# Moving layer norms and one inverse in a two-block transformer kernel: places in cross-attention, self-attention and SyncE's queue

## The chip, the cores and the metric

The kernel runs on one core of a Trainium2 chip. The metric is device microseconds of one execution. Five engines work side by side and meet at semaphores: TensorE (PE; weight loads are listed apart as PEld), VectorE (DVE), ScalarE (ACT), GpSimd (POOL) and SyncE (SP, which here only issues DMAs). Each runs its own list of instructions in order. In the profile SPq and ACTq are DMA-issuing instructions of SP and ACT.

## The reference

All of it is float32, x is 8 batches of 512 rows of 256. Two blocks follow each other; the change is in the second:

```python
attn_in = _adaln(x, cond, ln1_w, ...)      # layer norm, then (1 + g) * . + b from cond
x = _attn(attn_in, attn_in, sa_wq, sa_wkv, sa_wo, sa_bo) + x      # 16 heads of 64, rope on q and k
cross_in = _adaln(x, cond, ln1_w, ...)
ctx_n = _ln(context, ca_lnc_w, ca_lnc_b)   # 64 context rows of 192 per batch
x = _attn(cross_in, ctx_n, ca_wq, ca_wkv, ca_wo, ca_bo) + x
ffn_in = _adaln(x, cond, ln2_w, ...)
h = gelu(ffn_in @ ff_w1 + ff_b1)
x = h @ ff_w2 + ff_b2 + x
```

Each `_attn` divides its softmax numerators by their sums. The kernel applies exp without a row maximum, sums the exponentials with matmuls, and multiplies by the inverse of the sums later.

## The kernel before, in words

All eight x[b] stay in SBUF as 128 x 4 x 256 (512 rows in 4 tiles of 128). Within the second block the order of every engine's instructions is the order of the Python calls (a manual schedule); only a few loads outside it (the weights w_ff1 and w_ff2, both listed as w_ff_w, L140) are put into SP's list by the planner, where their buffers come free.

**A norm and its way to PE.** Statistics, rstd (a power on POOL, L158) and the product z (L191 in pieces, L170 in one) are 128 rows by 256 columns; PE wants the columns on the partitions. `blocks_turned` (L410) transposes 32 x 32 blocks on DVE (L413), writes them to HBM with four DMAs (`turned_d`, L416) and reads them back with one (`z<-turned_d`, L418), both on SP. `modulated` (L424, hT at L427) applies scale and shift on ACT. `normed_in_pieces` (L431) gives the norm as three pieces: statistics of two tiles; statistics of the other two and rstd; the product. `add_row` (L446) adds a bias row to x on POOL afterwards.

**Self-attention** (`slots`, L1125) goes through batches b and, in each, through four groups g of four heads. Per group: scores, exponentials on ACT, sums of the exponentials (sm) on DVE and POOL, values, and `sums` (L1065): four matmuls, a copy den on ACT, a DMA to HBM (den_d) and one back as 128 x 16 (rec). One group later `inverse` (L1083) takes the reciprocal on DVE, writes it to HBM (rec_d) and fetches it spread over partitions (rb, four DMAs), and `scaled` (L1100) multiplies oT by rb, half on DVE, half on POOL. All of these DMAs are on SP, except for those of the last group of the last batch, which `queue` (L1062) puts on ACT. Within batch b the norm of batch b+1 runs in pieces at g = 0, 0 and 1, and its modulation (`turn`) at g = 2.

**Between self-attention and cross-attention** the lines after the loop set the order by hand: cross_values 1 to 3 (the values of the context, copied on ACT to a tile v, written by SP to HBM as v_d), the norms of batches 0 and 1, the last group's inverse, the output projection of the last batch (`last_out`, first heads 0 to 5 of 8 pairs, then 6 and 7, which need the last inverse), the first two pieces of batch 2's norm. The tiles v and the turned blocks share the tag "t" with two buffers. `load_vb(0)` fetches the values back as kv.

**Cross-attention** (`cross`, in `fast_path`, L1369 on) has for each batch b eight places j = 0 to 7. Each place holds one query matmul group, six ahead of its use (`queries(8*b + j + 6)`), with rope on DVE (L846, L847) and POOL (L851, L852). Around them:

- j = 0: sums(b-1, 1), score(b, 0), two `outer` (values by output weights, copied to vw on ACT), scaled(b-1, 0)
- j = 1: turn(b+1), two `outer`, inverse(b-1, 1)
- j = 2: the first query that reads the hT of batch b+1; load_kb(b+1), load_vb(b+1)
- j = 4: sums(b, 0), score(b, 1), scaled(b-1, 1)
- j = 5, 6, 7: cross_out(b-1, t) with t = 0; 1; 2 and 3; then rows_(b+2, n) with n = 0, 1, 2, the three pieces of the norm of batch b+2 (for b = 6 and 7: of the feed-forward's batches 0 and 1)
- j = 6 also, behind those: inverse(b, 0)

Here sums, inverse and scaled go the same way over HBM, with two den DMAs (L1290), one rec (L1292), one rec_d (listed as `rec<-rec`, L1299), eight rb (L1304) and four products p<-p,rb (L1311), the odd ones on DVE, the even ones on POOL. cross_out (`ps<-vw,p`) sums over eight p, those of half 1 last. PSUM banks of queries, outer, sums and cross_out go round in the order D, O, X, X.

## Time and profile before

| | |
|---|---|
| median of 3 runs | 2320.97 us (2315.08 to 2325.16) |
| profiled execution | 2323.46 us, of which the span is 2321.6 us |
| granted TensorE clock, mean | 0.989 |
| first block | to about 804 us |
| self-attention of the second block | 804 to 1731 us |
| transition | 1731 to 1770 us |
| cross-attention | 1770 to about 2065 us, then feed-forward to the end |

A line of the timeline reads: start, duration, engine and line, operation, out<-in, count, and in brackets how long the engine had been idle before and what released it. PE busy counts modelled ends of pipelined matmuls. One float32 matmul appears as two records.

### The profile page before, as it was taken

The numbers are of one execution on the slowest core, as the hardware profiler recorded it, in microseconds if no ns is written. First come the engines' busy times: TensorE is split into PE (matmuls) and PEld (weight loads), VectorE is DVE, ScalarE is ACT, GpSimd is POOL, SyncE is SP. The second block draws the span as 40 slices with busy tenths as digits, with TensorE's granted clock in tenths as the row PEclk, the third lists the DMA queues.
The fourth block names the chain that finished last, engine by engine and source line by source line (L and its number), as shares of the span: only waits on it lengthen the run. The fifth ranks groups of instructions, "written<-read, shape, count | busy, mean of one in ns | idle before, by whom it ended". The sixth has DMA issues, their size and how long they took to land.

```text
span 2321.6 us, 30915 instructions
## 1 busy us (share of the span) xinstructions
PE 2274.8 (98%) x12180; PEld 1153.6 (50%) x12180; DVE 1113.9 (48%) x1935; ACT 864.8 (37%) x1309; POOL 922.6 (40%) x584
## 2 busy tenths in 40 slices
PE   9999999999999999999999999999998899999998
PEld 4444554554545533434343434343444455567665
DVE  5676555565555454444444444444434554442220
ACT  4566455455542134242424242424241221221221
POOL 4652333333210056454545454545443444432110
PEclk9999999999999999999999999999999999999999
DMA  6120000000002001010101010101033333322221
GB/s 191 34 96 6 12 6 8 12 6 7 3 10 75 18 15 38 20 38 20 38 19 38 20 38 19 38 20 38 20 96 106 103 94 86 103 73 79 55 62 35
DMA packets 106267, 104.16 MB, mean 45 GB/s; under 512 B 39185, under 2 KB 80897, under 8 KB 106113
## 3 DMA queue, kind: packets, MB, share of 16 engines
q1 hardware_dynamic: 104632, 98.92, 14.9%
q8 instruction: 98, 1.61, 0.3%
q0 software_dynamic: 576, 2.10, 0.2%
q10 hardware_dynamic: 904, 1.07, 0.2%
q14 instruction: 57, 0.46, 0.1%
HBM read 79.96 MB, written 22.09 MB: 44 GB/s over the span
## 4 chain that ended last, share of the span: by engine, by line
PE 91%; DVE 3%; DMA 3%; POOL 1%; issue 1%; SPq 1%; ACT 0%; ACTq 0%; DVEq 0%; POOLq 0%
PE ps_P L88 40%; PE ps_B L88 30%; PE ps_X L88 7%; PE ps_S L88 5%; PE ps_D L88 4%; PE ps_O L88 2%; DMA z<-turned_d 1%; DMA turned_d<-hT 1%; PE ps_B L566 1%; DVE z L191 1%; SPq L416 1%; PE ps_B L406 1%; POOL var L557 1%; PE ps_B L598 1%; DVE hT L413 0%
## 5 line engine op out<-in xcount | busy, mean ns | idle before, releaser
L615 ACT ACTIVATE p<-ps_B 128x512 f32<-128x512 f32 x576 | 292.1, 622 | 163.8 <-PE ps_B L88 163.8
L1036 ACT ACTIVATE p<-ps_P 128x1024 f32<-128x1024 f32 x256 | 244.8, 1025 | 90.9 <-PE ps_P L88 90.9
L88 PE MATMUL ps_P<-q,k 32*128 32x512 f32 x2048 | 238.9, 600 | 1.4 <-DVE t L1015 1.4
L1045 POOL TENSOR_TENSOR sm<-sm,p 128x1024 f32<-128x1024 f32 x64 | 176.7, 2760 | 135.3 <-ACT p L1036 134.8
L88 PE MATMUL ps_B<-hT,w 128*128 128x512 f32 x512 | 226.9, 597 | 1.1 <-ACT hT L407 0.9
L88 PE MATMUL ps_P<-p,v 128*32 128x512 f32 x2048 | 226.4, 594 | 0.0
L158 POOL TENSOR_TENSOR rstd<-rstd,mhalf 128x4 f32<-128x4 f32 x49 | 52.0, 1061 | 314.3 <-DVE rstd L157 313.4
L1004 ACT COPY v<-ps_P 128x1024 f32<-128x1024 f32 x32 | 32.4, 1012 | 376.1 <-PE ps_P L88 376.1
L1045 DVE TENSOR_TENSOR sm<-sm,p 128x1024 f32<-128x1024 f32 x64 | 100.8, 1575 | 145.8 <-ACT p L1036 145.8
L88 PEld LDWEIGHTS ps_P<-q,k 32*128 32x128 f32 x2048 | 99.1, 184 | 139.2 <-issue 113.6
L88 PEld LDWEIGHTS ps_B<-hT,w 128*128 128x128 f32 x512 | 95.3, 190 | 127.3 <-issue 98.7
L88 PEld LDWEIGHTS ps_P<-p,v 128*32 128x32 f32 x2048 | 63.3, 110 | 158.3 <-issue 134.8
L1043 POOL TENSOR_TENSOR sm<-p 128x1024 f32<-128x1024 f32 x32 | 79.1, 2473 | 157.4 <-ACT p L1036 157.4
L88 PE MATMUL ps_B<-q,k 16*128 16x512 f32 x1024 | 140.3, 617 | 1.2 <-DVE k L570 1.2
L557 POOL TENSOR_TENSOR var<-var,mhalf 128x32 f32<-128x32 f32 (+1 forms) x17 | 87.9, 5168 | 105.2 <-DVE var L551 98.2
L1014 DVE TENSOR_TENSOR t<-ps_P,rope_c 128x1024 f32<-128x1024 f32 x64 | 78.4, 1224 | 98.6 <-POOL q L1018 58.4
L88 PE MATMUL ps_B<-p,h 128*32 128x512 f32 x1024 | 119.6, 606 | 0.0
L1043 DVE TENSOR_TENSOR sm<-p 128x1024 f32<-128x1024 f32 x32 | 39.2, 1225 | 166.3 <-ACT p L1036 166.3
L88 PE MATMUL ps_P<-hT,w_sa_wq 128*128 128x512 f32 x256 | 118.3, 605 | 0.0
L88 PE MATMUL ps_P<-w_sa_wo,oT 128*128 128x256 f32 x512 | 114.0, 383 | 3.7 <-DVE oT L1103 2.1
L609 POOL TENSOR_TENSOR attn<-attn,gate 128x256 f32<-128x256 f32 x32 | 23.5, 735 | 232.8 <-DVE attn L607 231.8
L88 PE MATMUL ps_P<-hT,w_sa_wk 128*128 128x512 f32 x256 | 115.1, 592 | 0.0
(245 smaller groups left out, 3723.9 us busy)
## 6 DMA issues: line engine op xcount, KB each, us to landing
rb<-rec SPq DMA_DIRECT2D x128, 128.0 KB
rb<-rec_d SPq DMA_DIRECT2D x124, 128.0 KB
z<-turned_d SPq DMA_DIRECT2D x24, 512.0 KB
turned_d<-hT SPq DMA_DIRECT2D x60, 128.0 KB
turned_d<-t SPq DMA_DIRECT2D x36, 128.0 KB
out_dram<-x SPq DMA_DIRECT2D x15, 256.0 KB
x<-in_x_dram SPq DMA_DIRECT2D x7, 512.0 KB
gate<-modd SPq DMA_DIRECT2D x24, 128.0 KB
```

What stands on the lines that cost most here:

```text
L88: nc.tensor.matmul(o, lhsT, rhs, start=start, stop=stop)
L158: nc.gpsimd.tensor_tensor(r[:, :n], r[:, :n], mhalf[:, :n], ALU.pow)
L191: nc.vector.tensor_scalar(d[:, t, :width], x[:, t, :], s["mv"][:, t, 0:1], s["r"][:, t : t + 1], ALU.subtract, ALU.mult)
L406: nc.tensor.transpose(ps[:, t * P : (t + 1) * P], z[:, t, k * P : (k + 1) * P], ident)
L557: nc.gpsimd.tensor_tensor(var, var, half, ALU.pow)
L609: nc.gpsimd.tensor_tensor(attn, attn, gate.to_broadcast([P, NT, 4, HD0]), ALU.mult)
L615: nc.scalar.activation(p[i], ps, AF.Exp, scale=HD0 ** -0.5)
L1004: nc.scalar.copy(s["v", half][:, t0 : t0 + 2, :], ps)
L1014: nc.vector.tensor_tensor(c, ps, rope_c[:, None, :].to_broadcast([P, 2, N]), ALU.mult)
L1036: nc.scalar.activation(pr, pss[u], AF.Exp, scale=HD1 ** -0.5)
L1043: eng.tensor_tensor(s["sm", g, u], s["p", g, 0, u], s["p", g, 1, u], ALU.add)
L1045: eng.tensor_tensor(s["sm", g, u], s["sm", g, u], s["p", g, kt, u], ALU.add)
```

## The change

The changed kernel does five things. The norm of batch 0 for cross-attention becomes a class `First`, which stands in as the "next batch" of the last batch of self-attention, so that its pieces run within batch 7. The norm of batch 1 and the first two pieces of batch 2's norm move from behind `last_out((6, 7))` to in front of it. The last group's sums and inverse use SP like all others, and `inverse` stands between cross_values 1 and 2. `cross_values(3)` and `load_vb(0)` stand behind the norm of batch 1. In cross-attention rows_(b+2, 0 to 2) run at j = 4, 5, 6 instead of 5, 6, 7, in front of inverse(b, 0) at j = 6. In the changed kernel's SP list the load of w_ff2 stands in front of `kv<-v_d`; before it stood behind it.

```diff
-            def queue(self, g):
-                return nc.scalar if (self.b, g) == (B - 1, NG - 1) else nc.sync
...
             def sums(self, g):
...
-                self.queue(g).dma_start(dd, den.rearrange("(j r) n -> j r n", j=4)[:, 0, :])
-                if (self.b, g) != (B - 1, NG - 1):
-                    self.sums_back(g)
-
-            def sums_back(self, g):
-                s = self.s
+                nc.sync.dma_start(dd, den.rearrange("(j r) n -> j r n", j=4)[:, 0, :])
                 s["rec", g] = rec = wk.tile([P, 4 * N // P], F32, tag="rec", name="rec")
-                self.queue(g).dma_start(rec, flat(s["dd", g]))
+                nc.sync.dma_start(rec, flat(s["dd", g]))
 
             def inverse(self, g):
...
-                if (self.b, g) != (B - 1, NG - 1):
-                    self.inverse_back(g)
-
-            def inverse_back(self, g):
-                d = self.s["inv", g]
                 for u in range(2):
...
+        class First:
+
+            def __init__(self):
+                self.pieces = normed_in_pieces(nk, 0, EPS1, first_rows.append)
+
+            def norm(self, n):
+                self.pieces[n]()
+                if n == 2:
+                    first_rows.append(blocks_turned(by_way(), first_rows.pop()))
+                    add_row(0, row("cabo"))
+
+            def turn(self):
+                first_rows.append(modulated(rows_tile(nk), first_rows.pop(), 0, a1, b1))
...
-                nxt = todo[b + 1] if b + 1 < B else None
+                nxt = todo[b + 1] if b + 1 < B else First()
...
             end = todo[-1]
-            first_rows.append(blocks_turned(by_way(), normed(nk, 0, EPS1)))
-            add_row(0, row("cabo"))
             cross_values(wk, 1)
-            end.sums_back(NG - 1)
-            cross_values(wk, 2)
-            end.s["ps"] = [half[:, i, 0:D] for half in (pair(), pair()) for i in range(2)]
             end.inverse(NG - 1)
+            cross_values(wk, 2)
+            first_rows.append(blocks_turned(by_way(), normed(nk, 1, EPS1)))
+            add_row(1, row("cabo"))
             cross_values(wk, 3)
-            end.inverse_back(NG - 1)
             load_vb(0)
+            end.s["ps"] = [half[:, i, 0:D] for half in (pair(), pair()) for i in range(2)]
             end.last_out(range(6))
             end.scaled(NG - 1)
-            first_rows.append(modulated(rows_tile(nk), first_rows[0], 0, a1, b1))
-            end.last_out((6, 7))
-            first_rows.append(blocks_turned(by_way(), normed(nk, 1, EPS1)))
-            add_row(1, row("cabo"))
-
             ahead.extend(normed_in_pieces(nk, 2, EPS1, lambda z: turned_rows.update({2: z})))
             ahead[0]()
             ahead[1]()
+            end.last_out((6, 7))
...
-                    if j > 4:
-                        rows_(b + 2, j - 5)
+                    if 3 < j < 7:
+                        rows_(b + 2, j - 4)
                     if j == 6:
                         if b == B - 1:
                             sums(b, 1)
                         inverse(b, 0)
```

More of the change, by code (lines that the diff above doesn't have):

```diff
@@ L1085, in inverse @@
                 nc.vector.reciprocal(rec, rec)
-                self.s["inv", g] = d = dram.tile([4, N], F32, tag="rec_d", name="rec_d")
-                self.queue(g).dma_start(flat(d), rec)
+                d = dram.tile([4, N], F32, tag="rec_d", name="rec_d")
+                nc.sync.dma_start(flat(d), rec)
                 check(rec)
-                if (self.b, g) != (B - 1, NG - 1):
-                    self.inverse_back(g)
-            def inverse_back(self, g):
-                d = self.s["inv", g]
                 for u in range(2):
@@ L1096, in inverse_back @@
                     for e in range(2):
-                        self.queue(g).dma_start(rb[64 * e : 64 * e + 64, :],
+                        nc.sync.dma_start(rb[64 * e : 64 * e + 64, :],
                                                 d[2 * u + e : 2 * u + e + 1, :].to_broadcast([64, N]))
@@ L1149, in slots @@
                             jobs.append(lambda: this.values(1, 2 * g))
-                        if g == 2 and nxt:
+                        if g == 2:
                             jobs.append(nxt.turn)
-                    elif nxt:
+                    elif b + 1 < B:
                         jobs = [lambda: nxt.queries(0), lambda: nxt.keys(0), lambda: nxt.values(0, 0)]
@@ L1159, in slots @@
                             before[0].inverse(before[1])
-                        if n == 0 and nxt and g == 0:
+                        if n == 0 and g == 0:
                             nxt.norm(0)
@@ L1170, in slots @@
                     this.value(g)
-                    if nxt and g < 2:
+                    if g < 2:
                         nxt.norm(g + 1)
@@ L1177, in slots @@
             end = todo[-1]
-            first_rows.append(blocks_turned(by_way(), normed(nk, 0, EPS1)))
-            add_row(0, row("cabo"))
             cross_values(wk, 1)
-            end.sums_back(NG - 1)
+            end.inverse(NG - 1)
             cross_values(wk, 2)
+            first_rows.append(blocks_turned(by_way(), normed(nk, 1, EPS1)))
+            add_row(1, row("cabo"))
+            cross_values(wk, 3)
+            load_vb(0)
             end.s["ps"] = [half[:, i, 0:D] for half in (pair(), pair()) for i in range(2)]
-            end.inverse(NG - 1)
-            cross_values(wk, 3)
-            end.inverse_back(NG - 1)
-            load_vb(0)
             end.last_out(range(6))
             end.scaled(NG - 1)
-            first_rows.append(modulated(rows_tile(nk), first_rows[0], 0, a1, b1))
-            end.last_out((6, 7))
-            first_rows.append(blocks_turned(by_way(), normed(nk, 1, EPS1)))
-            add_row(1, row("cabo"))
             ahead.extend(normed_in_pieces(nk, 2, EPS1, lambda z: turned_rows.update({2: z})))
@@ L1201, in fast_path @@
     other_banks()
-    w_co, w_cq, ready = cross["o"], cross["q"], first_rows[1]
+    w_co, w_cq, ready = cross["o"], cross["q"], first_rows[0]
     extra.extend([bank_d, bank_o])
@@ L1211, in fast_path @@
         kvs.append((wk.tile([P, NPAIR, T], F32, name="kb", bufs=1), wk.tile([P, NPAIR, 2, T], F32, name="vb", bufs=1)))
-        turned_rows = {0: ready, 1: first_rows[2]}
+        turned_rows = {0: ready, 1: first_rows[1]}
         row_tiles = {1: rows_tile(wk)}
```

## The prediction

> **What bounds the kernel now.** I read the page first: the busy times, then the forty slices.

> ```profile
> PE 2274.8 (98%) x12180; PEld 1153.6 (50%) x12180; DVE 1113.9 (48%) x1935; ACT 864.8 (37%) x1309; POOL 922.6 (40%) x584
> PE   9999999999999999999999999999998899999998
> ```

> PE carries the kernel; its only two weak slices, at 1741 to 1857 us, hold the end of self-attention and the start of cross-attention, which the change touches. Next the waits of PE from 1731 us on (waiter, line, releaser; total, times, longest):

> ```profile
> PE ps_X L88 <- ACT hT L427: 20.1, 6, 6.3
> PE ps_O L88 <- DVE t L847: 4.2, 1, 4.2
> PE ps_S L88 <- ACT hT L427: 2.3, 1, 2.3
> PE ps_P L88 <- DVE oT L1103: 2.1, 1, 2.1
> PE ps_P L88 <- POOL oT L1103: 1.6, 1, 1.6
> ```

> That is 30.3 us. 22.4 us wait for modulated rows, once per batch (6.3, then 2.3 to 3.0); 7.9 us fall into the transition. What idling costs besides is in the windows (PE busy is the first number behind the length; granted clock third from the end):

> ```profile
> 1731.00:1770.00 39.00, 31.17 (x102) 20.53 (x101) 14.41 (x41) 5.14 (x6) 8.10 (x6) 0.93 0.51 155
> 1877.50:1917.60 40.10, 37.51 (x194) 22.57 (x193) 20.35 (x42) 8.69 (x12) 18.34 (x14) 1.00 0.36 94
> 1917.60:1959.40 41.80, 38.96 (x193) 23.15 (x193) 20.53 (x42) 8.69 (x12) 18.25 (x14) 0.96 0.33 91
> ```

> A cross batch is 37.5 us of PE at clock 1.00. It takes 40.1 us with one stall, and 41.8 us when the clock drops after it. The five from 1835.91 to 2041.41 average 41.1. The timeline of PE gives the stalls their places:

> ```profile
> 1738.66 10.53 PE L88 MATMUL ps_P<-w_sa_wo,oT 128*128 128x256 f32 x48
> 1751.26 0.70 PE L88 MATMUL ps_P<-w_sa_wo,oT 128*128 128x256 f32 x2 [2.08 <-DVE oT L1103]
> 1753.56 4.97 PE L88 MATMUL ps_P<-w_sa_wo,oT 128*128 128x256 f32 x14 [1.60 <-POOL oT L1103]
> ...
> 1768.70 2.05 PE L88 MATMUL ps_O<-w_ca_wo,kv 128*128 128x256 f32 x4 [4.15 <-DVE t L847]
> ...
> 1939.03 3.50 PE L88 MATMUL ps_X<-hT,w_ca_wq 128*128 128x512 f32 x4 [2.84 <-ACT hT L427]
> ```

> Last, SyncE's queue (issue times), which decides what replaces those stalls, and one line of VectorE:

> ```profile
> 1717.89 0.34 SPq L967 DMA_DIRECT2D v_d<-v  x1
> 1718.33 0.38 SPq L1087 DMA_DIRECT2D rec_d<-rec  x1
> 1722.72 2.39 SPq L1097 DMA_DIRECT2D rb<-rec_d  x4
> ...
> 1929.54 2.62 SPq L416 DMA_DIRECT2D turned_d<-hT  x4
> 1934.23 0.33 SPq L418 DMA_DIRECT2D z<-turned_d  x1
> 1934.66 1.10 SPq L1290 DMA_DIRECT2D den<-den  x2
> 1938.40 0.32 SPq L1292 DMA_DIRECT2D rec<-den  x1
> 1940.39 0.33 SPq L1299 DMA_DIRECT2D rec<-rec  x1
> 1941.86 4.97 SPq L1304 DMA_DIRECT2D rb<-rec  x8
> ```

> ```profile
> 1910.83 0.69 DVE L1311 TENSOR_TENSOR p<-p,rb 128x512 f32<-128x512 f32 x1 [1.66 <-DMA rb<-rec]
> ```

> The last multiply by an inverse waits for its rb, and cross_out(b-1,0) starts on PE at 1908.80 and reads that product (k=7) about 3.0 us in (14 of 16 records in 3.62 us): it is just in time today.

> **Part 1: transition.** Batch 0's norm goes into batch 7 of self-attention, as every earlier batch did for its successor: about 5.1 us of DVE (1727.23 to 1733.45 less the wait for rstd), 1.5 of ACT (two hT), 3.4 of POOL (rstd 1.02, add_row 2.36), five DMAs. PE idled 0.5 us in 884 to 1731 us with the same load in batches 0 to 6, so it costs nothing there; without that cover it would be those 5.1 us of DVE once.
> The last inverse: den is copied at 1728.45 to 1729.04. On ACT its steps stood behind copies of v that waited for buffers (5.11 and 5.13 us), so rb was issued at 1744.28. On SP: den_d 1729.1, rec about 1730.8 (1.70 later, as at 1710.28 and 1711.98), v_d at 1733, rec_d at 1733.5; behind a v_d it took 4.39 us to rb (above), against 1.47 us alone (1940.39 to 1941.86). So rb goes out at 1738 to 1740.5 and is multiplied by 1744. PE needs it at 1749.2, the end of the 48 records: 5 us of cover. The two waits go, and the 16 records run in 3.45 us at full clock: last_out ends at 1752.65 instead of 1758.53, saving 5.9 us.
> The 4.15 us stall came from DVE doing batch 1's norm and batch 2's statistics in front of the ropes. Both now stand before last_out((6,7)); it goes, with the 3.1 us that the slow matmuls behind it cost (two outers and a query took 1768.70 to 1775.28, 6.6 us; at full clock they take 0.87 + 0.87 + 1.73).
> A new wait: in the built order the load of w_ff2 (which waits for PE's last use of w_so) stands in front of kv<-v_d on SP. Before, kv went out at 1751.67, ahead of it. Now w_ff2 goes at 1752.7, kv at 1753.1 to 1754.4, and lands behind 1 MB, which took 2.6 us of traffic at 1758.57. I put landing at 1757.3. The first outer needs kv 3.4 us into cross-attention (1758.37 to 1761.80), at 1756.05: 1.2 us of stall, 0 to 4. Sum: 5.9 + 4.15 + 3.1 - 1.2 = **12.0 us** gained (8 to 13).

> **Part 2: the loop.** rows_(b+2, 2) runs at j=6 behind cross_out(b-1,1), not at j=7 behind cross_out(b-1,(2,3)). That is 8.64 us of PE earlier (1.73 query, 6.91 cross_out). hT was 2.3 to 3.0 us late; its rows would be about 6 us early, and ACT, which turns them behind two vw copies (end 1933.38), has the first half 0.8 us later, about 2 us before PE asks (1936.2). So the stall and the clock loss go: at most 41.1 - 37.5 = 3.6 us a cycle.
> But the five DMAs of rows_ also move in front of inverse(b,0) on SP. Count from t1, the end of cross_out(b-1,1) (1917.59): add, z and transpose put turned at +3.3 (1926.25 to 1929.54 today), z at +8.0, rec_d at +8.4. What z does to rec_d is not shown; den behind z waited 3.74 us from its issue, against about 1.5 for rec_d alone. I take 3.4 (bounds 1.5 and 4.4), since den is the nearest row: rb at +11.9, eight rb 5.1, then den(b,1) at +17.0.
> First consequence: scaled(b,0) at the next j=0. DVE's second product follows the first rb issue by 7.5 us (1903.09 to 1910.83, 2065.16 to 2072.70), so it ends at +20.2, and query 8b+7's rope behind it at +21.4. That rope frees ps_D, which the query at j=3 writes at +20.2 of PE: about 1.2 us of stall.
> Second: inverse(b,1). den 1.1 and 2 to land, reciprocal 1.65, rec_d 0.4, rb 1.47 (in three of seven batches 2.8 to 3.7), 7.5 to the second product and 0.7 for it: +31.9, or +33.5 in the slower kind. PE reaches k=7 at +31.7. The waits overlap, so a cycle pays about 1.2 and 1.8 in turn: 39.0 us. Five cycles: 5 x (41.1 - 39.0) = **10.5 us** (0.6 to 3.6 each: 3 to 18).
> [...]
> The statistics at j=4 and 5 now stand behind scaled(b-1,1) on DVE. After its second product come statistics 1.0, rope 1.2, q on POOL 2.5, rstd 1.0: 5.7 us; z starts 6.3 us after it (k=7 to t1 5.7, add 0.6), so rstd is in time by 0.6, and a later rb delays both alike.
> Batch 1: rows_(2,2) gains only the 1.7 us of one query (b=0 has no cross_out) plus the reciprocal and rope that stood before it: hT(2)'s wait falls from 6.3 to about 2.6. But the first cycle is short, and cross_out(0,0) reaches k=7 some 29 us after its t1, where the inverse is there at 34 to 35: 5 to 6 us of new wait. Net -2.5 (-5 to +2). Batch 7 and the feed-forward: hT(8)'s 2.3 us go, about 1 us each is paid at cross_out(6) and cross_out(7): +0.5.

> **Sum.** 12.0 + 10.5 - 2.5 + 0.5 = 20.5 us. The profiled execution had a span of 2321.6 us and took 2323.46, so 2303.0 there; it lay 2.5 us above the median of 2320.97, from which I predict 2300.5.

> **Rivals.** *PE's own work is all that is left* (cycle 37.5): for it, DVE and POOL are busy half of a cycle and rec_d alone takes 1.5 us; against it, the product already is just in time. 12 + 5 x 3.6 + 2 + 2.5 = 34.5: 2286.5. Chance 0.15.
> *The inverse takes the place of hT* (cycle 40.5): if the slower kind of rec_d holds in every cycle and rb lands a microsecond later. Batch 1 then loses 4: 12 + 3 - 4 = 11: 2310. Chance 0.17. hT still late, because ACT turns it no earlier, gives nearly the same time; its 2 us of margin speak against it: 0.02.
> *Slower*: the same loop with every small write behind bulk at v_d's price: rec_d 4.4, den 4.4 instead of 2, the second rec_d 3.7. Five to six us more make a cycle 43.5; the transition keeps 9 with kv at its worst, batch 1 loses 8 and the end 2: 9 - 8 - 5 x 2.4 - 2 = -13, 2334. With the rest as forecast (10 us gained) the sign turns from a cycle of about 43.1 on. Only v_d's 256-byte pieces show such a price: 0.06.
> The forecast has 0.60, its own range 2293 to 2307.

> **Numbers.** The range 2287 to 2312 takes in the floor's neighbourhood and the replacement, and leaves out the slower case and the tails. About 0.5% (11.6 us) is what a measurement of this kernel can tell from no change, so faster means below 2309.4: 0.58 of the forecast, 0.15 of the floor, 0.07 of the replacement: 0.80. Same 0.13, slower 0.07.

> **What would show it.** In the profile after: no PE wait on oT (L1090 after); last_out without a gap; a short PE wait on kv at the first outer; no PE wait on hT except near batch 2; turned_d and z in front of rec_d in SP's order, with rec_d to rb near 3.4 us; small PE waits at ps_D on the rope and at cross_out on p; cycles near 39.0 us at clock 1.00. Waits on hT of 2 us or more in every cycle, or cycles over 41 us, would make it wrong.

## The result, and the profile after

The changed kernel takes 2307.92 us (median of 8 runs, 2305.96 to 2310.70); the kernel before, on the same chip, 2321.25 us (8 runs, 2315.08 to 2329.00). The ratio is 0.9942, 95% interval 0.9924 to 0.9959: 13.3 us faster, where 20.5 were forecast. The profiled execution took 2307.98 us, with a span of 2306.2 us, so spans may be compared with times here: 2321.6 to 2306.2 is 15.4 us, 2.1 more than between the medians, as the profiled execution before was 2.2 us above its own.

Two rows of the page of the kernel after, busy times and PE's forty slices:

```profile
PE 2267.1 (98%) x12180; PEld 1148.8 (50%) x12180; DVE 1109.8 (48%) x1935; ACT 865.2 (38%) x1309; POOL 921.8 (40%) x584
PE   9999999999999999999999999999999899999999
```

PE is busy 7.7 us less with the same 12180 records: part of the gain is clock (granted 0.989 before, 0.993 after), not idle time. Of three slices below 9 one is left (the prediction spoke of two weak ones; the last slice, the end of feed-forward, is an 8 too in the kernel before). PE's waits from 1725 us on, in the kernel after:

```profile
PE ps_D L88 <- DVE t L847: 15.9, 6, 6.9
PE ps_X L88 <- DMA kv<-v_d: 4.3, 1, 4.3
PE ps_X L88 <- ACT hT L427: 2.3, 1, 2.3
PE ps_D L88 <- POOL p L1306: 0.7, 1, 0.7
```

30.3 us of waits became 23.2. The waits on oT and the one at ps_O are gone, and one wait on hT is left of seven; a wait on kv, six at ps_D on a rope and one on p are new. Their places, in PE's timeline:

```profile
1738.37 13.98 PE L88 MATMUL ps_P<-w_sa_wo,oT 128*128 128x256 f32 x64
1760.10 1.15 PE L88 MATMUL ps_X<-w_ca_wo,kv 128*128 128x256 f32 x4 [4.32 <-DMA kv<-v_d]
1761.04 3.57 PE L88 MATMUL ps_D<-hT,w_ca_wq 128*128 128x512 f32 x4
...
1812.44 3.54 PE L88 MATMUL ps_D<-hT,w_ca_wq 128*128 128x512 f32 x4 [6.91 <-DVE t L847]
...
1932.90 1.96 PE L88 MATMUL ps_D<-hT,w_ca_wq 128*128 128x512 f32 x4 [2.11 <-DVE t L847]
```

last_out is one block of 64 records. The query at 1761.04 takes 3.57 us where the same four records take 1.96 at 1932.90: half clock (granted 0.50 from 1761.02 to 1764.43). SyncE's queue in the kernel after, at the transition and in one cycle, with VectorE's reciprocal and what it then waited for:

```profile
1752.38 0.38 SPq L140 DMA_DIRECT2D w_ff_w<-in_ff_w_dram  x1
1752.81 1.26 SPq L955 DMA_DIRECT2D kv<-v_d  x2
...
1913.80 2.65 SPq L416 DMA_DIRECT2D turned_d<-hT  x4
1919.49 0.33 SPq L418 DMA_DIRECT2D z<-turned_d  x1
1919.86 0.43 SPq L1294 DMA_DIRECT2D rec<-rec  x1
1923.38 4.96 SPq L1299 DMA_DIRECT2D rb<-rec  x8
```

```profile
1913.69 0.31 DVE L1292 RECIPROCAL rec<-rec 128x32 f32<-128x32 f32 x1
...
1928.32 0.74 DVE L1306 TENSOR_TENSOR p<-p,rb 128x512 f32<-128x512 f32 x1 [3.09 <-DMA rb<-rec]
1930.87 0.69 DVE L1306 TENSOR_TENSOR p<-p,rb 128x512 f32<-128x512 f32 x1 [1.81 <-DMA rb<-rec]
1931.48 0.68 DVE L846 TENSOR_TENSOR t<-ps_D,rope_c 128x512 f32<-128x512 f32 x1
```

Read from the bottom: PE waits at 1932.90 for a bank that the rope of 1931.48 frees; the rope stands behind the two products, which wait for rb; rb goes out 3.52 us after rec_d. rec_d itself, whose reciprocal is done at 1914.00, goes out at 1919.86, 5.9 us later, since on SP it stands behind turned_d and z.

To place the gain, I cut each profiled execution at four points of PE: start of last_out, score(0,0), score(2,0) and score(7,0) (us; the five cycles are batches 2 to 6):

| kernel | up to last_out | last_out to score(0,0) | to score(2,0) | five cycles | score(7,0) to end |
|---|---|---|---|---|---|
| before | 1738.7 | 41.0 | 65.8 | 205.5 | 270.6 |
| after | 1738.4 | 33.9 | 68.4 | 196.8 | 268.7 |
| gain | 0.3 | 7.1 | -2.6 | 8.7 | 1.9 |

### The profile page after: what moved, and what is told of

It is laid out like the page before. It is cut to its first block, busy times and chain, and to the rows that moved or that the text cites. A ratio compares the mean times of both kernels' runs of the same rounds, so it can differ in the third digit from the quotient of the medians.

```text
span 2306.2 us, 30911 instructions
## 1 busy us (share of the span) xinstructions
PE 2267.1 (98%) x12180; PEld 1148.8 (50%) x12180; DVE 1109.8 (48%) x1935; ACT 865.2 (38%) x1309; POOL 921.8 (40%) x584
## 4 chain that ended last, share of the span: by engine, by line
PE 89%; DMA 4%; DVE 3%; SPq 2%; POOL 1%; issue 1%; ACT 0%; DVEq 0%; POOLq 0%; ACTq 0%
PE ps_P L88 41%; PE ps_B L88 30%; PE ps_S L88 5%; PE ps_X L88 4%; PE ps_D L88 4%; PE ps_O L88 2%; SPq L1299 1%; DMA rb<-rec 1%; DMA rec<-rec 1%; PE ps_B L566 1%; DMA turned_d<-hT 1%; POOL var L557 1%; PE ps_B L406 1%; DVE z L191 1%; PE ps_B L598 1%
## 5 line engine op out<-in xcount | busy, mean ns | idle before, releaser
L88 PE MATMUL ps_P<-q,k 32*128 32x512 f32 x2048 | 238.9, 600 | 1.4 <-DVE t L1015 1.4
L88 PE MATMUL ps_B<-hT,w 128*128 128x512 f32 x512 | 226.8, 597 | 1.1 <-ACT hT L407 0.9
L88 PE MATMUL ps_P<-p,v 128*32 128x512 f32 x2048 | 226.4, 594 | 0.0
L88 PEld LDWEIGHTS ps_P<-q,k 32*128 32x128 f32 x2048 | 99.1, 184 | 139.2 <-issue 113.6
L88 PEld LDWEIGHTS ps_B<-hT,w 128*128 128x128 f32 x512 | 95.3, 190 | 127.2 <-issue 98.7
L88 PEld LDWEIGHTS ps_P<-p,v 128*32 128x32 f32 x2048 | 63.3, 110 | 158.3 <-issue 134.8
L88 PE MATMUL ps_B<-q,k 16*128 16x512 f32 x1024 | 140.3, 617 | 1.2 <-DVE k L570 1.2
L88 PE MATMUL ps_B<-p,h 128*32 128x512 f32 x1024 | 119.6, 606 | 0.0
L88 PE MATMUL ps_P<-hT,w_sa_wq 128*128 128x512 f32 x256 | 118.3, 605 | 0.0
L609 POOL TENSOR_TENSOR attn<-attn,gate 128x256 f32<-128x256 f32 x32 | 23.5, 735 | 232.8 <-DVE attn L607 231.8
L88 PE MATMUL ps_P<-hT,w_sa_wk 128*128 128x512 f32 x256 | 115.1, 592 | 0.0
L88 PE MATMUL ps_P<-w_sa_wv,hT 128*128 128x512 f32 x256 | 114.9, 592 | 0.0
```

The lines of the kernel that those rows point to most:

```text
L88: nc.tensor.matmul(o, lhsT, rhs, start=start, stop=stop)
L609: nc.gpsimd.tensor_tensor(attn, attn, gate.to_broadcast([P, NT, 4, HD0]), ALU.mult)
```

## The experiments

The theory that they test: in the loop, what is left is SP's order (the inverse behind turned_d and z, which through rb holds DVE, and through the rope's bank PE); in the transition, it is kv behind a 1 MB load. The rivals: VectorE's own load, hT that is still the bound, or a gain that comes from the two parts only together.

### The two parts apart

Loop only: the kernel before, with this edit alone.

```diff
-                    if j > 4:
-                        rows_(b + 2, j - 5)
+                    if 3 < j < 7:
+                        rows_(b + 2, j - 4)
```

> The kernel before with only the three norm pieces of cross-attention moved from j = 5, 6, 7 to j = 4, 5, 6. If the loop's share is what the two traces show (five cycles from 41.1 to about 39.4 us, 2.5 us in batch 1, about 1.9 us behind the loop), the time is 2321 - 12 to 13 = about 2309, with the transition's two waits on oT still in the chain and no wait on hT in cycles 2 to 6. The predicted split (12.0 us from the transition, 8.5 from the loop) would give about 2312.5 here. If the loop's gain hangs on the transition (an earlier norm of block 1 lets hT(2) come sooner), 2315 or more. In all cases the waits at ps_D on the rope should be there, about 2 us in a cycle: they come from this part alone.

Transition only: the kernel after with those lines turned back.

> The kernel after with the norm pieces put back to j = 5, 6, 7: the transition's part alone. By the two traces score(0,0) starts 7.1 to 7.4 us sooner with it, 0.3 of which is drift: the time should be about 2321 - 7 = 2314, with the wait of 4.3 us on kv still there and the cycles back at 41.1 us with their waits on hT. By the prediction's sum for this part (12.0) it would be 2309. If the sooner start is lost in batch 1, where the wait on hT(2) would take it up, 2318 to 2321.

Loop only took 2313.15 us (12 runs, 2307.11 to 2319.91; ratio 0.9962, 0.9950 to 0.9973), transition only 2314.24 us (7 runs; 0.9971, 0.9960 to 0.9983), beside 2321.54 of before. The product of the two ratios is 0.9933, inside the interval of the whole change: the parts add. The transition is worth about 7 us, as its trace said, not 12.0. For the loop 2309 was expected from the two traces and 2313 came, which is near the 2312.5 of the prediction's own split. Where the 4 us went, the windows of one cycle show (length, PE busy; the granted clock is third from the end). First the loop-only kernel, then the kernel after:

```profile
1902.76:1943.95 41.19, 39.07 (x196) 22.88 (x193) 19.66 (x43) 8.80 (x12) 18.30 (x14) 0.96 0.36 92
```

```profile
1896.24:1935.79 39.55, 37.44 (x197) 22.53 (x193) 20.91 (x43) 8.81 (x12) 18.36 (x14) 1.00 0.38 96
```

Both cycles hold a wait of 2.1 us at ps_D. In one of them it is followed by half clock (0.96 over the cycle, for 1.00), which costs 1.6 us more. In the loop-only profile this happened in three of five cycles, in that of the kernel after in none.

### The load in front of kv

```diff
-        w_f2 = load_w("ff_w2", 3)
...
                         load_vb(b + 1)
+                        if b == 0:
+                            w_f2 = load_w("ff_w2", 3)
```

> The kernel after with one load moved: the second feed-forward weights (w_ff2, 512 KB) are issued behind load_vb(1) in batch 0 of cross-attention in place of in front of the fetch of kv. Theory: kv waits on SP's queue behind that load, and the 4.3 us at outer(0,0) with the slow clock behind it (matmuls of 0.87 us for about 0.47) are the term that the prediction had at 1.2. Then kv lands before outer(0,0) or within 1 us of it, score(0,0) comes 5 to 7 us sooner, and the time is 2301 to 2303. Rival: kv's 256-byte pieces take their 6.5 us by themselves; the wait stays above 3 us and the time within 1 us of 2308. A second rival: the start is sooner, but batch 1 gives it back, since there PE waits for a rope that DVE takes up late; the wait of 6.9 us at ps_D would grow to 11 to 13 and the time stay near 2308.

The time was 2305.38 us (5 runs, 2301.54 to 2310.57; ratio to before 0.9925, 0.9912 to 0.9938), above the expected 2301 to 2303 and not told apart from the change as it is. (The load is 1 MB, not the 512 KB that I wrote.) But the trace shows the mechanism: the chain that ended last has kv's fetch, from its second issue on, at 6.52 us in the kernel after and then at 3.31 us in this run.

```profile
1753.45 6.52 DMA kv<-v_d
```

```profile
1757.20 3.31 DMA kv<-v_d
```

The wait fell from 4.32 to 0.22 us, and last_out to score(0,0) from 33.9 to 28.1 us: 5.8 us, the 4.1 of wait and 1.7 of clock. The profiled execution, the longest of the five, does not show it in its total: it had half clock behind the rope waits of batches 2 and 5 (cycles of 41.3 and 41.7 us), and had reached last_out 4.7 us later than the kernel after. The other four left no trace.

### The inverse in front of turned_d and z

At j = 5, ahead of the norm piece:

```diff
+                    if j == 5:
+                        inverse(b, 0)
                     if 3 < j < 7:
                         rows_(b + 2, j - 4)
-                    if j == 6:
-                        if b == B - 1:
-                            sums(b, 1)
-                        inverse(b, 0)
+                    if j == 6 and b == B - 1:
+                        sums(b, 1)
```

> The kernel after with inverse(b,0) issued at j = 5 in front of the norm piece, where it stood at j = 6 behind it: on SP its store and its eight fetches of rb then go ahead of turned_d and z. Theory: the waits at ps_D (6.9 us in the first cycle, 1.2 to 2.5 in the others) come from rb, which stands behind z on SP, through DVE, which is held in scaled(b,0). Then these waits go; DVE waits about 2 us for rec at j = 5, beside PE's work; z is issued 1 to 2 us later, so hT keeps most of its 1.2 us of slack (a wait of up to 1 us on hT, 3 to 4 in batch 1), and the time is 2294 to 2299, the cycle 37.5 to 38.2. Rival: the waits come from DVE's load at j = 0 to 3 and not from rb; then ps_D's waits stay near 2 us and the time near 2308. Rival: hT or the last inverse take the place (waits on hT or p of about 2 us in each cycle): 2305 to 2310.

2286.51 us (4 runs, 2284.62 to 2288.51; ratio 0.9853, 0.9839 to 0.9867): 21.4 us below the change as it is, more than I expected. All of PE's waits from 1725 us on, in this run:

```profile
PE ps_X L88 <- DMA kv<-v_d: 3.9, 1, 3.9
PE ps_X L88 <- ACT hT L427: 3.9, 1, 3.9
```

No wait at ps_D is left, neither the 6.9 us of batch 1 nor those of the cycles. SyncE in one cycle of it, and that cycle's window:

```profile
1891.49 0.33 SPq L1294 DMA_DIRECT2D rec<-rec  x1
1892.95 4.96 SPq L1299 DMA_DIRECT2D rb<-rec  x8
1898.18 2.61 SPq L416 DMA_DIRECT2D turned_d<-hT  x4
1903.41 0.33 SPq L418 DMA_DIRECT2D z<-turned_d  x1
```

```profile
1880.63:1917.82 37.19, 37.19 (x196) 22.64 (x193) 20.22 (x43) 8.80 (x12) 18.29 (x14) 1.00 0.41 109
```

rec_d to rb is 1.46 us in place of 3.52, and PE is busy for every one of 37.19 us. All five cycles read 37.19 or 37.20, 186.0 in all: 10.8 less than after. In batches 0 and 1 it gains another 5.4 and behind score(7,0) 2.0, while 4.8 us of the span's 23.5 lie ahead of last_out, where both kernels do the same (the last section tells what they are).

Is it the place j = 5, or the order on SP? Here the inverse stays at j = 6 and is only called first:

```diff
                     if j == 6:
-                        if b == B - 1:
-                            sums(b, 1)
                         inverse(b, 0)
+                    if 3 < j < 7:
+                        rows_(b + 2, j - 4)
+                    if j == 6 and b == B - 1:
+                        sums(b, 1)
```

> The kernel after with inverse(b,0) still at j = 6, only issued in front of the norm piece in place of behind it: its place in time is kept, its place on SP changes (store and fetches of rb ahead of turned_d and z). Theory (SP's order, not the place j): rec_d to rb takes about 1.5 us as in the run with the inverse at j = 5, in place of 3.5; the waits at ps_D go; z comes 4 us later than in the kernel after (1923.5 for 1919.5 in the cycle read there), lands some 3.8 us later, 1927.3, and hT is ready at 1928.8 where PE wants it at 1928.9: no wait or under 1 us in cycles 2 to 6; in batch 1 the wait on hT(2) grows from 2.3 to about 6.3 with a stretch of half clock behind it. Time 2289 to 2293. Rival: the sooner place is what helped; then rb still comes late, ps_D's waits stay above 1 us, and the time is 2300 or more.

2292.84 us (4 runs; ratio 0.9868, 0.9851 to 0.9885), inside what the theory gave. SyncE in a cycle of it, and the one wait on hT:

```profile
1903.03 0.33 SPq L1294 DMA_DIRECT2D rec<-rec  x1
1904.49 5.38 SPq L1299 DMA_DIRECT2D rb<-rec  x8
1909.96 2.60 SPq L416 DMA_DIRECT2D turned_d<-hT  x4
1914.62 0.33 SPq L418 DMA_DIRECT2D z<-turned_d  x1
```

```profile
1806.21 3.78 PE L88 MATMUL ps_X<-hT,w_ca_wq 128*128 128x512 f32 x4 [5.91 <-ACT hT L427]
```

Again 1.46 us from rec_d to rb, no wait at ps_D, cycles of 37.19 to 37.24. So the order decides, not the place j, and not VectorE's load either, which is the same work here. The new order also spares the reciprocal the 2.6 us of z and transpose on VectorE, but by the lines above the larger part was on SP: 5.9 us in front of rec_d and 2.1 more behind it. The sooner place spares batch 1 2 us on hT(2), since z goes out sooner there; of the 7.4 us between the two spans, 4.1 lie ahead of last_out.

The same move of the inverse to j = 5 in the kernel before:

> The kernel before with inverse(b,0) at j = 5 and nothing else: the norms stay at j = 5, 6, 7. Theory: the two edits work only together. Here z's chain still starts at j = 7, PE still waits 2.5 to 3 us for hT in every cycle (rb was not late in the kernel before, since it went ahead of turned_d), and the time is within 4 us of 2321. Rival: the inverse's place alone is worth the 21 us that it gave on top of the change: 2300 or less.

2318.98 us (11 runs; ratio 0.9992, 0.9978 to 1.0005), no difference. Its waits on hT stand as they were before:

```profile
PE ps_X L88 <- ACT hT L427: 19.4, 6, 5.3
```

Over the five cycles the inverse alone gains nothing (207.6 us for 205.5), the norm alone 4.8 (loop only, 200.7) to 8.7 (the kernel after), and both together 19.5 (186.0): the norm's sooner place opened the room, and the inverse behind it kept the change from filling it.

### Towards a better version

Both edits, the later load and the inverse at j = 5:

> The last load of feed-forward weights behind load_vb(1) and the inverse at j = 5, both. Theory: the parts add, since the sooner start of score(0,0) (5.8 us from last_out on, with the load moved alone) had been eaten only in part by slow-clock stretches behind the waits at ps_D, and these waits are gone: 2286.5 - 5.6 = 2281, with cycles of 37.2 us and one wait left, 3 to 4 us on hT(2) in batch 1. Rival: block 2's norm at j = 6 of batch 0 is fixed by something other than PE's pace, so that the wait on hT(2) grows by what was won: about 2286.

2283.59 us (5 runs, 2281.34 to 2290.00; ratio 0.9832, 0.9814 to 0.9850). That lies between the theory's 2281 and the rival's 2286; the waits are those of the theory. The transition takes 27.7 us, and one wait is left, 3.9 us on hT(2). From last_out to the end it takes 544.2 us, where the inverse alone takes 549.1; the medians differ by 2.9 and their intervals overlap. To take that last wait, block 2's last norm piece went to j = 2 of batch 0:

```diff
                         if b == 0:
+                            rows_(2, 2)
                             w_f2 = load_w("ff_w2", 3)
...
-                    if 3 < j < 7:
+                    if 3 < j < 7 and b:
```

> The kernel before this one in the list with block 2's last norm piece (its transpose, turned_d, z and the row) called at j = 2 of batch 0 in place of j = 6. Theory: the wait of 3.9 us on hT(2) and the 3.4 us of half clock behind it (1.7 us of time) go, and PE has no wait above 0.5 us from last_out to the first feed-forward: 2281 - 5.6 = 2275 to 2277. Rival: the work moved holds the ropes at j = 2 and 3 of batch 0, or the scaling of batch 0 at j = 0 of batch 1 waits on rb in place: a wait of 2 to 5 us there, 2279 to 2282.

2280.80 us (5 runs; ratio 0.9828, 0.9812 to 0.9844). The expected 2275 to 2277 was missed and the rival's price held. From last_out to the end its trace takes 545.0 us, no less than the 544.2 of the version before it; its span is shorter only because it reached last_out 4.1 us sooner. hT(2) is in time, but SyncE and VectorE of this run show a new cause, and PE's line its effect (its releaser is not named there; the next run tells it):

```profile
1778.51 0.39 SPq L140 DMA_DIRECT2D w_ff_w<-in_ff_w_dram  x1
1778.99 1.11 SPq L1284 DMA_DIRECT2D den<-den  x2
1784.75 0.33 SPq L1286 DMA_DIRECT2D rec<-den  x1
```

```profile
1786.44 0.35 DVE L1291 RECIPROCAL rec<-rec 128x32 f32<-128x32 f32 x1 [8.08 <-DMA rec<-den]
```

```profile
1788.41 2.34 PE L88 MATMUL ps_X<-w_ca_wo,vb 128*128 128x256 f32 x8 [3.13 <-issue]
```

The 1 MB load now stood in front of the sums of batch 0: the same mistake as with kv, one place on. So it went to the last batch, which loads no keys and values (`if j == 2 and b == B - 1:`):

> The run with block 2's norm piece at j = 2 again, with the load of w_ff2 (1 MB) moved on from batch 0 to j = 2 of the last batch, where no cross keys and values are loaded. Theory: there DVE stood 8.1 us in front of the reciprocal of batch 0, since the sums' way back stood behind that load on SP (5.8 us from the store of den to the issue of rec's fetch, for 2.3 elsewhere), and PE's wait of 3.1 us at 1788 (its bank waits for a rope queued behind the reciprocal on DVE) and of 2.0 us at ps_D come from it. Then both go or fall to under 1 us in sum, DVE waits 4 us or less, and the time is 2275 to 2277. Rival: DVE's order alone does it (a reciprocal one place behind its sums with no other work between them): the wait of 3 us stays, the time is 2280 or more.

2281.22 us (5 runs, 2277.10 to 2282.89; ratio 0.9824, 0.9801 to 0.9847). The wait of 3.1 us is gone; DVE waits 5.0 us for the sums, not the 4 or less that I gave, and 1.8 us are left at ps_D. From last_out to the end this execution takes 541.6 us, the shortest of all, 3.4 less than the run before it. The medians do not show that: the expected 2275 to 2277 was missed. Two runs of five came near it (2277.1 and 2277.5, clock 0.998), the other three (clock 0.995 and 0.996) took 2281 to 2283. These last three versions are not told apart by their times; each beats the kernel before by 1.5% to 2.0% and lies below the change as it is too.

## Why the prediction was right, and where its sum failed

The time lay inside the range and in the direction forecast, 7.4 us above the predicted 2300.5. It lay 0.9 us outside the forecast's own narrower range (2293 to 2307), and nearer to the 2310 of the second rival, the inverse in hT's place; by the time alone the two could not be told apart. The trace decides for the forecast: rec_d to rb at 3.5 us, cycles of 39.4 us and not 40.5, and most of what is missing lies in the transition. By the cuts, the terms came out so (us, gain):

| term | forecast | measured |
|---|---|---|
| transition | 12.0 | 7.1 |
| batch 1 | -2.5 | -2.6 |
| five cycles | 10.5 | 8.7 |
| batch 7 and feed-forward | 0.5 | 1.9 |
| ahead of last_out | 0 | 0.3 |
| sum | 20.5 | 15.4 |

**Transition: the step that failed.** Three of its four terms held: last_out runs without a gap, the ropes' stall is gone, and so are the slow matmuls behind it (5.9, 4.15 and 3.1). The fourth, "I put landing at 1757.3 ... 1.2 us of stall, 0 to 4", was mis-sized: the wait is 4.32 us, just past the end of the bounds. I had the order on SP right and took the 1 MB ahead of kv at its own traffic of 2.6 us. I gave kv hardly anything on top, but its own pieces take 3.3 us even without that load in front, as the moved load showed. And having charged half clock to the old stall, I charged none to the new one; the query of 3.57 us is 1.7 of it. 5.9 + 4.15 + 3.1 - 4.3 - 1.7 = 7.15, which is the measured 7.1.

**The loop: right mechanism, a little mis-sized.** rec_d behind z takes 3.52 us to rb (forecast 3.4) and 1.46 once it stands ahead. The chain rb, product, rope, bank, PE is the one forecast, and two runs removed it by putting the inverse in front of turned_d and z. The wait at ps_D is 1.2 to 2.5 us, 1.8 in the mean, where I had 1.2: z went out 8.0 us behind t1, as forecast, in three cycles, and 9.0 to 9.1 in the two with the longest waits; the second wait, on the last inverse at cross_out, was to raise that to 1.8 in some cycles and came once, with 0.7 us, behind the five. That PE's wait at ps_D made the inverse timely there is likely, but no run shows it alone. A cycle takes 39.4 us for the forecast 39.0.

My 3.4 was an estimate beside the 3.74 us of den behind z in the kernel before. The runs gave 3.37 to 3.54 us behind z in the five cycles of the kernel after, and 1.46 in front of it, with the same instructions. What in z's 512 KB holds rec_d up, they do not show.

**Batch 1: right sum, wrong place.** I looked for 5 to 6 us at cross_out(0,0). That was for the second inverse; the first one, for which I had put nothing at ps_D in this batch, already struck in the scaling at j = 0, as 6.9 us at ps_D. That the two are of a size is luck. With the inverse ahead, 5.4 us came back from score(0,0) to score(2,0).

**The end.** hT's wait of 2.3 us in front of the feed-forward went, and of the two waits on p that I set against it only the one of 0.7 us came.

**The rivals.** The floor, a cycle of 37.5 us and a time of 2286.5, was real but one edit away: 37.19 us and 2286.51 with the inverse moved. The cycle is the mechanism; that the times agree to the tenth is luck, since the floor's sum took 12.0 us from the transition, and it gives 7.5 there. hT was not the bound once the norm had moved, and no chain turned slower. The store of v_d behind which the slower rival read its 4.4 us has no 256-byte pieces: from 1717.9 to 1720.2 us in the kernel before, its 512 KB moved in packets of 2 to 8 KB, 126 of them. The small pieces are those of kv's fetch (1056 packets for 0.26 MB).

## What to carry to other kernels

Where a group of transfers is moved sooner on a queue, look at what it has been moved past: here a 16 KB store that a whole chain hangs on went behind 512 KB, which took back more than half of what the loop could give, and the order of two calls repaired it. A fetch behind a bulk load can cost both, the load's traffic and its own: here 6.5 us for 3.3. Cost a stall of PE at two values, bare and with the clock loss behind it (here 1.6 to 1.7 us for one stretch of 3.41 us at half clock), and compare kernels from a common anchor in the trace when the expected difference is a few microseconds.

## What the runs showed of the hardware

```profile
1856.00:1856.50 0.50, 0.00 (x0) 0.00 (x0) 0.00 (x0) 0.15 (x1) 0.50 (x1) 1.00 0.00 0
1856.50:1857.00 0.50, 0.00 (x0) 0.00 (x0) 0.00 (x0) 0.50 (x1) 0.24 (x1) 0.80 0.00 0
1857.00:1857.50 0.50, 0.29 (x1) 0.29 (x2) 0.00 (x0) 0.50 (x2) 0.00 (x0) 0.50 0.01 2
...
1860.00:1860.50 0.50, 0.50 (x2) 0.26 (x1) 0.00 (x0) 0.00 (x0) 0.00 (x0) 0.79 0.00 0
1860.50:1861.00 0.50, 0.50 (x3) 0.26 (x2) 0.29 (x1) 0.00 (x0) 0.00 (x0) 1.00 0.00 0
```

Laid over the waits of the five cycles, the grid gives the longest part of each wait inside one interval (us):

| kernel | batch 2 | 3 | 4 | 5 | 6 |
|---|---|---|---|---|---|
| before, wait | 2.69 | 2.59 | 2.84 | 3.01 | 2.64 |
| before, inside one interval | 2.28 | 1.62 | 2.53 | 1.67 | 2.16 |
| before, half clock behind it | yes | no | yes | no | yes |
| after, wait | 2.49 | 1.82 | 2.11 | 1.21 | 1.30 |
| after, inside one interval | 1.73 | 1.82 | 1.22 | 1.21 | 0.69 |
| after, half clock behind it | no | no | no | no | no |

The three waits with 2.16 us or more inside one interval were followed by half clock, the seven with 1.82 us or less were not, the longest of all (3.01 us, across an edge) among them. Outside the five cycles, in the kernel before, one interval from 1751.0 with 1.88 us in two waits was followed by half clock too. This was worked out from the traces; no run was made to test it. It would explain why equal waits of 2.1 us gave cycles of 39.55 and 41.19 us (that of the shorter cycle lies across an edge, 0.89 us before it and 1.22 behind), and some of the spread of one kernel's times: up to 172 us, where all kernels run the same code, the profiles of before and after hold four such stretches (one of double length) and that of the run with the inverse at j = 5 holds one, and last_out starts 4.8 us sooner in the latter. Why three executions of the last version took 4 to 6 us more than the other two was not seen: they left no trace.
